# Turning a routed tile by blocks: 32 by 32 loads and a VectorE transpose in place of a TensorE transpose and a copy

## Chip, core and metric

The kernel runs on one core of a Trainium2 chip. All times are device microseconds of that core. The profile is one execution of the program with the hardware profiler on; the time before is the median of three further runs, 540.95 us (540.62 to 541.41).

## The reference

A block with two gated parts, over 8 batches of 256 tokens with 256 features, all in fp32:

```python
x = x + tanh(g_xattn) * xattn(layernorm(x), ctx)      # 16 heads of 64, 120 context rows
x = x + tanh(g_ffn) * ffn(layernorm(x))               # 8 experts, the best 2 of each token

# ffn
probs = softmax(x @ Wr.T)                    # (B, T, 8)
topk_vals, topk_idx = top_k(probs, 2)
gate = one_hot(topk_idx) weighted by topk_vals / topk_vals.sum()
h = silu(einsum('btd,efd->btef', x, W1))     # 256 -> 1024 for every expert
y = einsum('btef,edf->bted', h, W2)          # 1024 -> 256
out = einsum('bte,bted->btd', gate, y)
```

The change concerns only the way in which the expert part gets its rows.

## The kernel before

The attention part comes first: 32 units of half the heads by half a batch. Beside it the tokens of finished batches are routed. `router` finds the two best experts of each token, `places` gives each (token, expert) pair a row in a table in device memory, `routed`, which has one region of 2048 rows for each expert, and GpSimd sends the normalized token to both of its rows. A row has 265 floats: 256 features, 8 gates and the token's number, 1060 bytes.

The expert part works through `order`: eight "first" tiles, the first 128 rows of each expert's region (experts 0, 1, 2, 6, 3, 4, 5, 7 in this order), and then 23 "full" tiles, j = 8 to 30, whose expert and first row are read at run time from a small table that VectorE computes. For each tile, `load` brings 128 rows into a slot `xt` of 128 partitions by 265, one row to a partition. There are six such slots, and loads run four tiles ahead (`AHEAD`). Three other things can follow only on the slot: `turn`, the tile's gate, and the token numbers that the final addition needs.

`turn` makes the features lie on the partitions, which the first product needs: TensorE transposes each half of the tile into PSUM (two instructions, line 865) and VectorE copies both halves to `xT` in SBUF (line 867). `up` multiplies with the expert's first weights (line 874, 32 instructions of one tile) and ScalarE applies silu; `down` multiplies with the second weights (line 890, 16 instructions); VectorE scales by the gate (line 898); GpSimd adds the result to `out` through a list of row numbers (line 915). Each such addition waits for the one before it. For a full tile VectorE also copies the expert's two slabs of weights from the resident `w_sb` (lines 845 and 854) and one gate (line 850).

Small remainders of an expert's rows are worked in "quads", four lots of 32 rows to a tile; two of them run between the full tiles 16 to 23, and they keep their own load (GpSimd's gather, line 821).

The order on TensorE, VectorE, ScalarE and SyncE is the order of the program text (`manual_schedule`), so each of these engines takes its instructions strictly in turn. In the steady state an iteration i of the main loop issues, on TensorE, `up` of tile i, the turn of tile i+1, and `down` of tile i-1. On VectorE it issues the slab copy, gate copy and turn of tile i+1, then the second slab of tile i and the scaling of tile i-1.

SyncE (SP) is the queue of all tile loads of the first and full kind, and also of the stores of `x` and of the experts' weights: `load_expert(e)` sends two transfers of 1 MB (lines 407 and 410). The weights of experts 6, 5, 4, 3 and 7 can only be loaded when the attention part has left their room in `w_sb`, so they come at the change from one part to the other. In the last batch's four steps k = 0 to 3 the kernel loads the first four tiles, all at k = 0:

```python
if n == B and k == 0:
    for i in range(AHEAD):
        xts[i] = load(order[i])
```

The order on SP from there is: loads of tiles 0, 1, 2, 6; store of x of batch 6; weights of experts 6, 5, 4; load of tile 3; store of x of batch 7; load of tile 4; weights of 3 and 7; loads of tiles 5 and 7; then the full tiles. A transfer on SP carries one of eight completion semaphores in rotation, and it is issued only when the transfer eight places before it, which had the same semaphore, has landed.

Of the kernel before, what the change touches and what calls it, by code (L numbers as in the profile page):

```python
# [15 lines left out]
P = 128  # L16
B, N, D = 8, 256, 256
# [4 lines left out]
T = B * N  # L22
# [4 lines left out]
DC = D // P  # L27
# [8 lines left out]

EARLY = 2
QUARTER = 32
FULLS = 31
SPARE = 8  # L40
QUADS = 6
# [7 lines left out]
def tile_gated_xattn_moe(  # L49
# [15 lines left out]
    nc = tc.nc  # L65
# [6 lines left out]
    fp = ctx.enter_context(tc.tile_pool(name="ffn", bufs=2))  # L72
# [15 lines left out]
    routed = tc.dram_tile([E * T + P, XW], F32, name="routed")  # L88
# [35 lines left out]
    for e in range(E):  # L124
# [4 lines left out]

    places_w = const.tile([P, FULLS], F32, name="places_w")  # L130
    nc.gpsimd.iota(
        places_w, [[1, FULLS]], base=-FULLS, channel_multiplier=0,
        allow_small_or_imprecise_dtypes=True,
# [23 lines left out]
    def quarters_places():  # L157
# [4 lines left out]
        nc.vector.scalar_tensor_tensor(  # L162
            lane, quarter_i, float(-QUARTER), number[:, 0:1], ALU.mult, ALU.add
        )
# [45 lines left out]
    behind = []  # L210
    firsts = []
# [440 lines left out]
    def row(tag, n, dtype=F32):  # L652

        if tag in ("expert_i", "full_row", "quad_row", "own", "experts_i", "more_i"):
            return fw[3].tile([P, n], dtype, tag=tag, name=tag, bufs=1)
        if not scratch:
            scratch.append(fw[0].tile([P, FC * D], F32, tag="w2", name="scratch"))
            scratch.append(0)
        a, scratch[1] = scratch[1], scratch[1] + n
        r = scratch[0][:, a : a + n]  # L660
        return r if dtype == F32 else r.bitcast(dtype)
# [47 lines left out]
    def table():  # L709
# [15 lines left out]
        )  # L725
        nc.vector.tensor_scalar(tails, left, float(P - QUARTER), None, ALU.is_gt)
        nc.vector.tensor_scalar(begin[:, E:], first_row, float(P), None, ALU.add)
# [4 lines left out]

        at = row("at", FULLS)
        nc.vector.tensor_scalar(at, places_w, upto[:, 2 * E - 1 :], None, ALU.add)
        used = row("used_w", FULLS)
        nc.vector.tensor_scalar(used, at, 0.0, None, ALU.is_ge)
        yield
        which, first = sought("w", at, upto, counts, begin, P)
        full_row = row("full_row", FULLS, I32)
        where(first, used, full_row)  # L740
        expert_i = row("expert_i", FULLS, I32)
        nc.vector.tensor_scalar(used, which, float(E), float(-E), ALU.is_ge, ALU.mult)
# [5 lines left out]
        for k in range(1, 3):  # L748
            nc.vector.scalar_tensor_tensor(
                quarters, left, float(k * QUARTER), quarters, ALU.is_gt, ALU.add  # L750
            )
# [5 lines left out]
        nc.vector.tensor_scalar(used, places_q, upto_q[:, E - 1 :], None, ALU.is_lt)  # L757
        which, first = sought("q", places_q, upto_q, quarters, begin[:, :E], QUARTER)
        where(first, used, first)
# [40 lines left out]
    def take(pool, shape, tag, name, dtype=F32, **kw):  # L800
        if spare is None:
            return pool.tile(shape, dtype, tag=tag, name=name, **kw)
        key = tag, *shape
        if key not in spare:
            spare[key] = pool.tile(shape, dtype, tag=tag, name=name, **kw)
        return spare[key]


    def load(t):
        kind, i = t  # L810
        xt = take(fp, [P, XW], "xt", f"xt_{kind}{i}", bufs=6)
        if kind == "first":
            first = nc.sync.dma_start(xt, routed[ds(i * T, P), :])
            for send in behind:
                tc.declare_no_dep(
                    first.ins, send.ins, reason="rows behind those of the first tiles"
                )
            firsts.append(first)
            return xt
        if kind == "quad":  # L820
            nc.gpsimd.indirect_dma_start(
                out=xt,
                out_offset=None,
                in_=routed[:, :],
                in_offset=bass.IndirectOffsetOnAxis(
                    ap=tables[1][0][:, i : i + 1], axis=0
                ),
            )
            return xt
        start = nc.sync.value_load(  # L830
            tables[0][1][0:1, i : i + 1], min_val=0, max_val=NOWHERE
        )
        nc.sync.dma_start(xt, routed[ds(start, P), :])
        return xt

    def weights(t, xt):

# [22 lines left out]
        return w1, gate, copy_w2  # L860

    def turn(t, xt):
        tr = take(ps_tr, [P, DC, P], "tr", f"xtT_{t[0]}{t[1]}")
        for c in range(DC):
            nc.tensor.transpose(tr[:, c, :], xt[:, ts(c, P)], ident)
        xT = take(fp, [P, DC, P], "xT", f"xT_{t[0]}{t[1]}")
        nc.vector.tensor_copy(xT, tr)
        return xT
# [73 lines left out]
    def quad(j, xt):  # L942
# [30 lines left out]
        for h in range(2):  # L973
# [4 lines left out]
            for c in range(DC):  # L978
                for q in range(4):
                    nc.tensor.matmul(  # L980
                        pu[ts(q, QUARTER), :],
                        lhsT=xT[:, c, ts(q, QUARTER)],
                        rhs=w[:, q, ts(c, 512)],
# [41 lines left out]
    def open_tile(t, xt):  # L1025
        state["ready"] = t, xt, weights(t, xt), turn(t, xt)
# [11 lines left out]
    order = [("first", e) for e in (0, 1, 2, 6, 3, 4, 5, 7)]  # L1038
    order += [("full", j) for j in range(SPARE, FULLS)]
    mix = 16  # L1040
    AHEAD = 4
    xts = {}
# [35 lines left out]
    for s, (b, o, nb) in enumerate(units):  # L1078
        k = 2 * o + nb
        n = b + 1  # L1080
        g = b // 2 - 1
        routing = b > 1 and b % 2 == 1
        if s + 1 < len(units):
            prs[s + 1] = scores(units[s + 1])

        if s == 0 or k == 2 and b + 2 < B:
            norms_x.finish()
        if k == 0 and b > 1:
            norms_y.finish()
        if k == 1 and b + 2 < B:  # L1090
            if b > 1:
                xs[b + 2] = load_x(b + 2)
            norm_x(b + 2)
        if k > 1 and b > 0:
            norm_y(b - 1, k - 2)


        copies, sums = [], []
        if k == 0 and b > 0:
            weigh(b - 1, 1, ps_mm)  # L1100
        if k == 1 and routing:
            lg = logits(g, groups[g][1], bank_mm)
            next(lg)
        if k == 2:
            weigh(b, 0, ps_mm)
            if b > 0:
                sums.append(wide_out(b - 1, 1, ps_mm))
        if k == 0:
            project_q(b, xnTs[b], 3)
            if n < B:  # L1110
                project_v(b, int(b == 0))
        elif n < B:
            project_q(n, xnTs[n], k - 1)
        if k == 1:
            copies += next_k(b, 0)
            if routing and n < B:
                lg = next(lg)
            if b > 0:
                sums.append(wide_out(b - 1, 0, ps_mm))
            if routing and n == B:  # L1120
                lg = next(lg)
        if k == 3:
            copies += next_k(b, 1)
            if b > 0:
                project_v(b, 1)
            if n == B - 1:
                project_v(n, 0)
        if b == 1 and k % 2 == 0:
            copies.append(project_kk(2, k))
        for copy in copies:  # L1130
            copy()
        if s + 1 < len(units):
            divide(*prs[s + 1])
        if k == 0 and b > 1:
            turn_y(b - 2, bank_mm)


        if routing and n < B and k == 1:
            picked[g] = router(g, lg)
        for add in sums:  # L1140
            add()
        if routing and n < B and k == 2:
            sending[g] = places(g, groups[g][0], picked[g], bank_mm)
            if g == EARLY - 1:
                fill_firsts()
        if n < B:
            for step, each in list(sending.items()):
                if s < 8 * step + 18:
                    next(each)
        if s == 7:  # L1150
            quarters_places()
        if b == 0 and k == 2:
            nc.vector.tensor_scalar(bias_sb, bias_sb, tg[:, 0:1], None, ALU.mult)
        if s in (3, 4):
            bias_x(s - 3)
        if k == 1 and 0 < b < B - 1:
            bias_x(n)
        if n == B and k == 0:
            for i in range(AHEAD):
                xts[i] = load(order[i])  # L1160
        if n == B and k == 3:
            open_tile(order[0], xts[0])
            picked[g] = router(g, lg)
        turn_pr((b, o, nb), *prs.pop(s))
        if k == 3 and b + 2 < B:
            turn_x(b + 2)
        if s == 0:
            turn_x(1)
        if k == 3 and b in (2, 3, 4):
            load_expert(b - 2)  # L1170
        if k == 3 and n == B:
            load_expert(6)
# [18 lines left out]
    for i, t in enumerate(order):  # L1191
        if i == 12:

            with tc.If(more > 0):  # L1194
                spare = {}
                for j in range(SPARE):
                    tj = ("full", j)
                    xt = load(tj)
# [126 lines left out]
```

## Time and profile before

| | before |
|---|---|
| median of 3 runs | 540.95 us |
| profiled execution | 540.71 us |
| its span | 538.9 us (1.8 us lie around it) |
| TensorE busy | 525.8 us, 98% |
| VectorE busy | 285.1 us, 53% |
| ScalarE busy | 219.8 us, 41% |
| GpSimd busy | 128.7 us, 24% |
| DMA, mean share of the 16 engines, 270 to 310 us | 0.95 |
| the same, 335 to 405 us | 0.24 |

In the profile's rows, "out<-in" names the tiles written and read, "xN" counts instructions, and the number after the bar is the busy time with the mean duration of one. Durations of consecutive TensorE instructions overlap, so 46 instructions with a mean of 273 ns can be busy for 8.8 us. "Idle before" is the time that the engine stood still ahead of a group, and the name behind the arrow is what ended it. SPq is SyncE's queue; its rows show how long an issue took, and "to landing" counts from the issue to the completion.

### The profile page before, as it was taken

What the parts mean: (1) busy time and instruction counts of PE and PEld (TensorE: products, weight loads), DVE (VectorE), ACT (ScalarE), POOL (GpSimd) and SP (SyncE); (2) the same over time, 40 slices, a digit from 0 to 9 for tenths busy, and PEclk for the clock granted to TensorE, in tenths of its full rate; (3) what the DMA queues carried; (4) which work ended last, traced back from release to release, by engine and by line L of the source; (5) the groups of instructions that cost most, each with busy time, mean ns of one, the idle gap of its engine ahead of it and who ended that gap; (6) DMA issues with size and microseconds to landing.
All of it is one profiled execution on the core that took longest, in us unless ns stands there. A gap on an engine that the chain in (4) does not pass through costs nothing. (4 is left out here: it accounts for less than half of the span.)

```text
span 538.9 us, 9932 instructions
## 1 busy us (share of the span) xinstructions
PE 525.8 (98%) x3698; PEld 444.8 (83%) x3698; DVE 285.1 (53%) x683; ACT 219.8 (41%) x700; POOL 128.7 (24%) x135
## 2 busy tenths in 40 slices
PE   8999999999999999999999999999999999999992
PEld 7788887878878788787889999998997878889991
DVE  3675656567765677645663447444453453543530
ACT  1666546464664645557530311011144635501110
POOL 2011100000332003310014473222322124343422
PEclk9999999999999999999999999999999999999997
DMA  8999980140521401111099932312221210321311
GB/s 299 337 309 298 309 246 21 51 144 2 177 79 47 171 1 40 42 52 31 1 316 328 308 90 63 50 30 44 38 43 21 41 34 7 51 46 12 50 22 19
DMA packets 46439, 57.53 MB, mean 107 GB/s; under 512 B 3184, under 2 KB 41456, under 8 KB 46384
## 3 DMA queue, kind: packets, MB, share of 16 engines
q1 hardware_dynamic: 39488, 47.35, 28.6%
q0 software_dynamic: 6480, 8.81, 9.2%
q8 instruction: 32, 0.52, 0.4%
q10 hardware_dynamic: 416, 0.66, 0.4%
q14 instruction: 23, 0.19, 0.1%
HBM read 28.67 MB, written 28.27 MB: 106 GB/s over the span
## 5 line engine op out<-in xcount | busy, mean ns | idle before, releaser
L574 ACT ACTIVATE pr<-psc,mx 128x120 f32<-128x120 f32 x256 | 88.4, 372 | 64.5 <-DVE mx L568 64.5
L874 PEld LDWEIGHTS ph_full<-xT_full,w 128*128 128x128 f32 x736 | 85.0, 192 | 6.5 <-issue 5.7
L874 PE MATMUL ph_full<-xT_full,w 128*128 128x128 f32 x736 | 86.8, 276 | 0.3 <-PEq L1194 0.3
L890 PE MATMUL py_full<-w,hT_full 128*128 128x256 f32 x368 | 83.1, 379 | 0.0
L890 PEld LDWEIGHTS py_full<-w,hT_full 128*128 128x128 f32 x368 | 68.2, 190 | 8.4
L882 ACT ACTIVATE hT_full<-ph_full 128x1024 f32<-128x1024 f32 x23 | 23.5, 1023 | 97.7 <-PE ph_full L874 97.7
L524 PE MATMUL pq<-xnT,w_sb 128*128 128x256 f32 x256 | 62.7, 388 | 0.4 <-DVE xnT L207 0.4
L915 POOL DMA_INDIRECT out_dram<-y_full,xt_full x23 | 39.0, 1697 | 99.8 <-DVE y_full L898 70.4
L618 PE MATMUL pw<-w_sb 128*128 128x256 f32 x256 | 58.5, 382 | 0.0
L574 ACT ACTIVATION_READ_ACCUMULATOR pr<-psc,mx 128x1 f32 x256 | 55.7, 218 | 0.0
L524 PEld LDWEIGHTS pq<-xnT,w_sb 128*128 128x128 f32 x256 | 46.6, 190 | 10.8 <-issue 3.1
L618 PEld LDWEIGHTS pw<-w_sb 128*128 128x128 f32 x256 | 47.7, 190 | 9.0 <-issue 2.5
L562 DVE TENSOR_REDUCE mx<-psc 128x8 f32<-128x960 f32 x32 | 37.0, 1156 | 31.1 <-PE psc L554 31.1
L365 POOL DMA_INDIRECT routed<-rows,slot x32 | 32.1, 1002 | 54.4 <-DVE slot L361 47.4
L594 ACT COPY w_sb<-tr 120x512 f32<-120x512 f32 x64 | 34.6, 597 | 20.1 <-PE tr L593 20.1
L583 DVE TENSOR_TENSOR pr<-pr,sm 128x960 f32<-128x960 f32 x32 | 37.1, 1158 | 1.1
L554 PE MATMUL psc<-kT,w_sb 64*128 64x120 f32 x512 | 37.2, 284 | 0.0
L898 DVE TENSOR_SCALAR y_full<-py_full,gate 128x256 f32<-128x256 f32 x23 | 11.1, 484 | 48.5 <-PE py_full L890 44.8
L962 ACT COPY part<-w_sb 128x1024 f32 x32 | 31.1, 1043 | 14.1 <-PE py_q L1001 13.5
L554 PEld LDWEIGHTS psc<-kT,w_sb 64*128 64x128 f32 x512 | 31.1, 187 | 6.4 <-issue 3.6
L593 PEld LDWEIGHTS tr<-ident,pr 128*120 128x120 f32 x256 | 29.5, 138 | 5.5 <-issue 2.5
L845 DVE COPY w<-w_sb 128x2048 f32 x23 | 28.8, 1251 | 9.5 <-issue 4.3
(177 smaller groups left out, 670.6 us busy)
## 6 DMA issues: line engine op xcount, KB each, us to landing
routed<-w_sb SPq DMA_DIRECT2D x8, 2120.0 KB, 21.4
w_sb<-in_w1T_dram SPq DMA_DIRECT2D x8, 1024.0 KB, 5.7
w_sb<-in_w2T_dram SPq DMA_DIRECT2D x8, 1024.0 KB, 9.9
xt_full<-routed SPq DMA_DIRECT2D x23, 132.5 KB, 2.1
out_dram<-x SPq DMA_DIRECT2D x8, 256.0 KB, 2.4
x<-in_x_dram SPq DMA_DIRECT2D x7, 256.0 KB, 2.8
w_sb<-in_w_kv_dram SPq DMA_DIRECT2D x3, 512.0 KB, 8.0
xt_first<-routed SPq DMA_DIRECT2D x8, 132.5 KB, 2.5
```

The costliest lines, as they stand in the source:

```text
L365: send = nc.gpsimd.indirect_dma_start(out=routed[:, :], out_offset=bass.IndirectOffsetOnAxis(ap=slot[:, i : i + 1], axis=0), in_=rows[h][: ...
L524: nc.tensor.matmul(pq[:, i, :], lhsT=wq_sb[:, c, ts(2 * h + i, P)], rhs=xnT[:, c, :], start=(c == 0), stop=(c == DC - 1),)
L554: nc.tensor.matmul(psc[:, j, ts(i, M)], lhsT=qT[ts(j, DH), 4 * o + i, ts(nb, P)], rhs=kT[ts(j, DH), 4 * o + i, :], start=True, stop=True,)
L562: nc.vector.tensor_reduce(mx.rearrange("p (j i) -> p j i", i=4), psc[:, :, : 4 * M].rearrange("p j (i m) -> p j i m", m=M), AX.X, ALU.max,)
L574: nc.scalar.activation(pr[:, h, :], psc[:, j, ts(i, M)], AF.Exp, bias=mx[:, h : h + 1], scale=QK_SCALE, accum_out=sm[:, h : h + 1],)
L583: nc.vector.tensor_tensor(pr, pr, sm.unsqueeze(2).to_broadcast([P, 8, M]), ALU.mult)
L594: nc.scalar.copy(pT_sb[:, ts(j, 4), ts(nb, P)], tr[:M, :, :])
L618: nc.tensor.matmul(pw[:, :D], lhsT=oT_sb[b % 2][:, ci, ts(k, P)], rhs=wo_sb[:, ci, :], start=(ci == 0), stop=(ci == IC - 1),)
L874: nc.tensor.matmul(ph[:, f, :], lhsT=w1[:, c, ts(f, P)], rhs=xT[:, c, :], start=(c == 0), stop=(c == DC - 1),)
L890: nc.tensor.matmul(py[:, :D], lhsT=hT[:, f, :], rhs=w2[:, f, :], start=(f == 0), stop=(f == FC - 1),)
L915: add = nc.gpsimd.indirect_dma_start(out=out[:, :], out_offset=bass.IndirectOffsetOnAxis(ap=slots[:, k : k + 1], axis=0), in_=y[own, :], i ...
L962: nc.scalar.copy(w[:, q, :].rearrange("p (a b) -> p a b", b=D if down else DFF // 2), slab[:, ts(h, FC // 2), :] if down else slab[:, :, t ...
```

## The change

The features of a first or full tile are no longer loaded with one transfer of 128 rows. `load_blocks` issues eight transfers: for each 32 features out of each half, the 128 rows' 32 floats go to the 32 partitions on which those features will lie after the turn, as four blocks of 32 rows by 32 floats side by side. A ninth transfer brings the gates and the token numbers (9 floats) of each row. VectorE's transpose, which turns each 32 by 32 block in its place, then makes `xT` out of the slot with one instruction, SBUF to SBUF. TensorE's two transposes, the PSUM bank and the PSUM copy are gone for these tiles; quads keep them. The four loads of the last batch's k = 0 are spread: one tile's at each k.

```diff
@@ load(t)
         if kind == "first":
-            first = nc.sync.dma_start(xt, routed[ds(i * T, P), :])
-            for send in behind:
-                tc.declare_no_dep(...)
-            firsts.append(first)
+            for first in load_blocks(xt, i * T):
+                for send in behind:
+                    tc.declare_no_dep(...)
+                firsts.append(first)
             return xt
...
-        nc.sync.dma_start(xt, routed[ds(start, P), :])
+        load_blocks(xt, start)
         return xt
+
+    def load_blocks(xt, start):
+        loads = []
+        for k in range(P // BLK):
+            for c in range(DC):
+                loads.append(
+                    nc.sync.dma_start(
+                        xt[ts(k, BLK), ts(c, P)].rearrange("s (b r) -> s b r", r=BLK),
+                        routed[ds(start, P), ds(c * P + k * BLK, BLK)].rearrange(
+                            "(b s) r -> s b r", s=BLK
+                        ),
+                    )
+                )
+        loads.append(nc.sync.dma_start(xt[:, D:], routed[ds(start, P), D:]))
+        return loads
...
     def turn(t, xt):
+        if t[0] != "quad":
+            xT = take(fp, [P, DC, P], "xT", f"xT_{t[0]}{t[1]}")
+            nc.vector.transpose(xT.rearrange("p c n -> p (c n)"), xt[:, :D])
+            return xT
         tr = take(ps_tr, [P, DC, P], "tr", f"xtT_{t[0]}{t[1]}")
...
-        if n == B and k == 0:
-            for i in range(AHEAD):
-                xts[i] = load(order[i])
+        if n == B:
+            xts[k] = load(order[k])
```

`BLK` is 32. The order of VectorE's and TensorE's instructions is otherwise the same.

More of the change, by code (lines that the diff above doesn't have):

```diff
@@ L38 @@
 QUARTER = 32
+BLK = 32
 FULLS = 31
@@ L812, in load @@
         if kind == "first":
-            first = nc.sync.dma_start(xt, routed[ds(i * T, P), :])
-            for send in behind:
-                tc.declare_no_dep(
-                    first.ins, send.ins, reason="rows behind those of the first tiles"
-                )
-            firsts.append(first)
+            for first in load_blocks(xt, i * T):
+                for send in behind:
+                    tc.declare_no_dep(
+                        first.ins, send.ins, reason="rows behind those of the first tiles"
+                    )
+                firsts.append(first)
             return xt
@@ L832, in load @@
         )
-        nc.sync.dma_start(xt, routed[ds(start, P), :])
+        load_blocks(xt, start)
         return xt
+    def load_blocks(xt, start):
[9 more added lines that the diff above has]
+                    )
+                )
+        loads.append(nc.sync.dma_start(xt[:, D:], routed[ds(start, P), D:]))
+        return loads
     def weights(t, xt):
```

## The prediction

> **What bounds the kernel now.** I read the page's first part, then TensorE by stretches, then its order in one tile. TensorE is busy for 98% of the span, and by stretches it has no holes where the tiles run:
>
> ```profile
> core 0: us, PE busy (x) PEld busy (x) DVE busy (x) ACT busy (x) POOL busy (x), PEclk, DMA share, GB/s
> 270.00:310.00 40.00, 39.92 (x282) 35.38 (x281) 18.44 (x76) 10.38 (x13) 13.10 (x15) 1.00 0.95 321
> 335.00:405.00 70.00, 69.65 (x474) 64.94 (x472) 33.33 (x60) 14.13 (x14) 18.60 (x12) 1.00 0.24 40
> ```
>
> So what TensorE no longer issues shortens the kernel, as long as nothing else arrives late. The second thing to see is the DMA share: 0.95 from 270 to 310 us, where five experts' weights come in, and 0.24 in the full tiles. The change takes work from TensorE and gives it to DMA and SP. TensorE's timeline around one turn:
>
> ```profile
> 331.67 3.73 PE L874 MATMUL ph_first<-xT_first,w_sb 128*128 128x128 f32 x32
> 335.24 0.38 PE L865 MATMUL xtT_full<-ident,xt_full 128*128 128x128 f32 x2
> 335.46 3.62 PE L890 MATMUL py_first<-w_sb,hT_first 128*128 128x256 f32 x16
> ```
>
> The columns are start and duration. The next product starts 0.22 us after the two transposes did (335.24 to 335.46), although each is drawn longer: 0.22 us is what they take from the path. A plain tile lasts 7.24 us (start of `up` to start of `up`).
>
> **TensorE.** 8 first and 23 full tiles are turned, 31 x 0.22 = 6.8 us removed. Nothing on TensorE replaces it, and `up` waits for the same `xT`.
>
> **VectorE.** Out goes one PSUM copy of 128x256 (423 ns, line 867), in comes one block transpose of the same size, which the trace does not show. Bounds: 367 ns, the SBUF normalization of line 196 (0.73 us for two), and 846 ns, if it takes two passes of the 423. I take 440, nearest the copy. [...] By any of these the sum gets 0: VectorE spends some 3.5 of 7.2 us on a tile, and stood 1.7 us before each such copy, waiting for TensorE:
>
> ```profile
> L867 DVE COPY xT_full<-xtT_full 128x256 f32<-128x256 f32 x23 | 9.7, 423 | 39.6 <-PE xtT_full L865 39.5
> ```
>
> That wait (39.5 us over 23) goes; what VectorE now waits for instead is the slot's landing, with line 854's slab, the scaling of line 898 and so the addition queued behind it.
>
> **SP.** One issue of a tile becomes nine. The trace has the 128x265 load at 333 ns, a store in three dimensions (line 641) at 383 ns. For a block I take 0.38, and with the address work that each full load shows (42 + 29 + 28 ns) 0.48: 9 x 0.48 = 4.3 us, and 0.9 us for reading the row number (325.9 to 326.8): 5.2 us of SP for a full tile, 3.8 for a first tile. Less than 7.0, and SP has little else to do there; it mostly waits for slots to come free:
>
> ```profile
> SPq L833 <- DMA out_dram<-y_full,xt_full: 113.0, 14, 20.5
> ```
>
> A slot was loaded 12.5 us or more before its tile's `up` from the twelfth tile on (the tightest: 498.20 to 510.72); a load of 4.3 + 2.1 us of landing still fits.
>
> **The load on the DMA engines.** 128 packets of 1060 bytes become 1024 of 128 bytes and 128 of 36, and each transfer adds 16 small ones: 1296 in all. No row has 128 bytes. From above: the plain loads at 327 to 331 us.
>
> ```profile
> q0 software_dynamic: 145, 0.13, 24.7%
> q1 hardware_dynamic: 272, 0.26, 23.5%
> ```
>
> q1 is two tile loads: 23.5% of 16 engines x 4 us = 15.0 us for 272 packets, 55 ns each. From below: 14.0 to 15.0 us into the run, where the router's weights come in rows of 32 bytes, in two halves:
>
> ```profile
> DMA packets 287, 0.16 MB, mean 323 GB/s; under 512 B 145, under 2 KB 272, under 8 KB 287
> q1 hardware_dynamic: 287, 0.16, 110.8%
> ...
> DMA packets 205, 0.14 MB, mean 287 GB/s; under 512 B 89, under 2 KB 190, under 8 KB 205
> q1 hardware_dynamic: 205, 0.14, 121.4%
> ```
>
> They are busy for (1.108 + 1.214) x 8 = 18.6 us. Half a microsecond of large packets just before (13.0 to 13.5) took 8.4 us for 0.19 MB, 44 us a MB; 0.30 MB at that price is 13.3, and 5.3 us over 234 small packets is 23 ns. On the line from 23 ns (32 bytes) to 55 (1060) 128 bytes cost 26. So a tile takes 1296 x 26 / 16 = about 2.1 us of all engines, at most 1296 x 55 / 16 = 4.5; before it was 0.5. At 2.1 SP's issue is the slower of the two.
>
> [...]
>
> **The crowded stretch.** SP's order around the weights (start, time of issue):
>
> ```profile
> 269.57 0.39 SPq L641 DMA_DIRECT2D out_dram<-x  x1
> 270.59 0.38 SPq L407 DMA_DIRECT2D w_sb<-in_w1T_dram  x1
> ...
> 279.27 0.72 SPq L410 DMA_DIRECT2D w_sb<-in_w2T_dram  x1
> 280.03 5.13 SPq L813 DMA_DIRECT2D xt_first<-routed  x1
> 290.59 0.38 SPq L641 DMA_DIRECT2D out_dram<-x  x1
> 291.40 0.34 SPq L813 DMA_DIRECT2D xt_first<-routed  x1
> 291.80 0.44 SPq L407 DMA_DIRECT2D w_sb<-in_w1T_dram  x1
> ```
>
> Spreading the first four loads puts tile 6's nine issues behind the store at 269.57: the weights start at 273.9 instead of 270.59. Expert 4's last slab (279.27, 13.0 us to landing) then lands at 295.6 instead of 292.3. Tile 3's blocks are each eight places behind a weight transfer, the eighth behind this slab; so the store of x waits until about 296.5, tile 4's nine follow, and expert 3's first slab is issued at about 301.3 instead of 291.80. Landing like expert 6's (5.0 us), it is there at 306.3. Its product stood at 309.63 and is now due 5 x 0.22 earlier, 308.5: 2.2 us of room, no stall. Further down, the late store delays the first additions and through them GpSimd's sends, the last of which the first full load waits for (327.76 before). I estimate 1.5 us later; with 4.3 us of issues and 2.2 to landing it is there at 335.8, VectorE's turn ends at 336.4, and `up` is due at 337.1. Nearly nothing is left, so I charge 0.5 us for stalls in this stretch (0 to 3).
>
> **The end.** The additions each wait for the one before (issue 1.55, then 2.98 us idle, some 4.5). Behind the second quad they form a chain that has caught up with TensorE only at 518.92. Blocks beside them may cost 1 us; the chain has 1.77 us of room at its last link but one. Charged 0.
>
> **The sum.** 540.7 (profiled) - 6.8 + 0.5 = 534.4; the median of the runs stands 0.2 above the profiled time: 534.6.
>
> **Rivals.** (1) *Late weights.* If a tile's load takes more than about 4.5 us, that is above 55 ns a packet, the 2.2 us of room is used up three times over (tiles 6, 3 and 4 lie ahead of expert 3's slab), and the first full tiles come late too. At 5.8 us: 3 x 1.3 = 4 us more, 538.5. For it: the share of 0.95; against: 23 ns for small packets. (2) *The loads become the bound, slower than before.* The place is the full tiles: a load of L us and the additions' share (16.4% of the engines from 360 to 400 us, 1.15 us a tile) must fit in 7.0 us. Otherwise the last of 23 loads lands at 327.8 + 3 (L - 4.5) + 23 (L + 1.15), and 18 us of last products and addition follow. [...] Against: both rows above. (3) *Nothing gained.* The 6.8 us are eaten by small stalls, or the chain of additions does not move with TensorE: 541. Against: TensorE sets the last four additions' time.
>
> **How the numbers follow.** As computed 0.56 (533.2 to 536.2 its own range), rival 1 0.15 (536 to 540), rival 3 0.06, rival 2 0.23 (542 to 575). A measurement tells 0.2%, 1.1 us, from no change. Faster: 0.56 + 0.15 less 0.01 at its end, 0.70; same 0.07; slower 0.23. The range begins at 533.0 (all 6.8 us, no stall, and 1 us of spread) and reaches into rival 2 until some 0.17 is left above: 550.
>
> **What would show it.** Right: no line 865 for first and full tiles, `up` to `up` in 7.02 us, a transpose under 0.65 us, nine issues in under 5 us, a tile's packets under 30 ns. Wrong: TensorE idle before `up` of tile 3 or of full tile 8 (VectorE waiting for a load), SP's issues longer than 0.7 us each, a DMA share near 1 in the full tiles.

## The result and the profile after

The changed kernel takes 538.01 us (median; single times from 536.65 to 540.82), the kernel before 540.9 us beside it. The ratio is 0.995, with a 95% interval of 0.993 to 0.997: a gain of 2.9 us, where 6.3 were forecast. The profiled execution took 538.01 us, its span is 536.3 us.

Most of the forecast's mechanics are in the trace. TensorE by stretches, in the profile after (columns as before: busy time and instructions of each engine, granted clock, DMA share, GB/s):

```profile
270.00:310.00 40.00, 40.00 (x285) 35.84 (x284) 19.82 (x85) 10.10 (x13) 13.13 (x15) 1.00 0.85 275
335.00:405.00 70.00, 69.70 (x476) 65.21 (x474) 32.59 (x60) 14.15 (x14) 18.57 (x12) 1.00 0.33 43
```

TensorE still has no holes in these two stretches, and the loads in blocks raise the DMA share in the full tiles from 0.24 to 0.33 only. TensorE's timeline around two full tiles of the kernel after:

```profile
480.22 3.73 PE L897 MATMUL ph_full<-xT_full,w 128*128 128x128 f32 x32
483.79 3.62 PE L913 MATMUL py_full<-w,hT_full 128*128 128x256 f32 x16
487.25 3.73 PE L897 MATMUL ph_full<-xT_full,w 128*128 128x128 f32 x32
```

`up` to `up` is 487.25 - 480.22 = 7.03 us, where it was 7.24. The turn is gone from TensorE. What VectorE does in its place, from the groups of the kernel after (busy time and mean ns, then the idle time before it with its releasers), with the scaling, line 898 before and 921 after:

```profile
L884 DVE STREAM_TRANSPOSE xT_full<-xt_full 128x256 f32<-128x256 f32 x23 | 10.0, 435 | 1.1 <-DMA xt_full<-routed 0.6 <-DVE gate L869 0.3 <-issue 0.2
L898 DVE TENSOR_SCALAR y_full<-py_full,gate 128x256 f32<-128x256 f32 x23 | 11.1, 484 | 48.5 <-PE py_full L890 44.8
L921 DVE TENSOR_SCALAR y_full<-py_full,gate 128x256 f32<-128x256 f32 x23 | 11.1, 483 | 61.6 <-PE py_full L913 55.7
```

The transpose takes 435 ns. The 39.6 us that VectorE stood ahead of the copy have shrunk to 1.1 ahead of the transpose; part of that idle time now lies ahead of the scaling, which waits for `down` (61.6 us, 48.5 before). On the pages of the kernel before and of the kernel after, the queue of the loads:

```profile
q1 hardware_dynamic: 39488, 47.35, 28.6%
q1 hardware_dynamic: 75200, 47.36, 31.9%
```

The difference is 0.319 x 16 x 536.3 - 0.286 x 16 x 538.9 = 271 us of engine time for 35712 packets more: some 8 ns for each packet that came on top. That is not what one packet costs, since the large ones are gone. The durations in the trace of the kernel after give that: a packet of 128 bytes takes 14.5 ns in the mean, one of 36 bytes 10.4, one of 4 bytes (16 to a transfer) 9.1. A tile's 1024, 128 and 144 of them make 17.5 us of engine time, 13.5 ns a packet, or 1.1 us of all 16 engines.

SP's order around the weights, from its timeline in the kernel after:

```profile
274.42 0.43 SPq L852 DMA_DIRECT2D xt_first<-routed  x1
274.95 0.39 SPq L408 DMA_DIRECT2D w_sb<-in_w1T_dram  x1
...
296.81 0.40 SPq L642 DMA_DIRECT2D out_dram<-x  x1
297.25 3.86 SPq L845 DMA_DIRECT2D xt_first<-routed  x8
301.16 0.43 SPq L852 DMA_DIRECT2D xt_first<-routed  x1
301.63 0.43 SPq L408 DMA_DIRECT2D w_sb<-in_w1T_dram  x1
```

The weights start at 274.95 (forecast 273.9), the store of x at 296.81 (296.5), expert 3's first slab at 301.63 (301.3). So the gain was there. It was lost again in one place. At 322.45 TensorE was 1.97 us ahead of the kernel before (the same `up` had begun at 324.42). The timeline of the kernel before, one line, and then that of the kernel after:

```profile
324.42 3.73 PE L874 MATMUL ph_first<-xT_first,w_sb 128*128 128x128 f32 x32
...
322.45 3.73 PE L897 MATMUL ph_first<-xT_first,w_sb 128*128 128x128 f32 x32
326.07 0.59 PE L913 MATMUL py_first<-w_sb,hT_first 128*128 128x256 f32 x2
326.86 0.46 PE L913 MATMUL py_first<-w_sb,hT_first 128*128 128x256 f32 x1 [0.20 <-issue]
328.27 0.59 PE L913 MATMUL py_first<-w_sb,hT_first 128*128 128x256 f32 x2 [0.95 <-issue]
329.69 1.20 PE L913 MATMUL py_first<-w_sb,hT_first 128*128 128x256 f32 x2 [0.83 <-issue]
331.10 3.19 PE L913 MATMUL py_first<-w_sb,hT_first 128*128 128x256 f32 x9 [0.21 <-issue]
334.13 3.73 PE L897 MATMUL ph_first<-xT_first,w_sb 128*128 128x128 f32 x32
```

One `down` (16 instructions) takes 334.13 - 326.07 = 8.06 us, where it takes 3.45. That is 4.6 us lost, in the middle of a product: its operands were there, and "issue" says that TensorE waited for nothing that the profile shows. Two things go with it. ScalarE's timeline in the same place ("remote" is a releaser that the profile could not name):

```profile
331.42 1.02 ACT L905 ACTIVATE hT_first<-ph_first 128x1024 f32<-128x1024 f32 x1 [10.03 <-remote]
```

The `up` that this silu waits for ended at about 326.1; the increment of TensorE's semaphore that announces it is recorded at 331.34, 5.2 us later. VectorE runs on meanwhile without a pause, until 330.7. And the granted clock (last column but two), by windows of 2 us:

```profile
328.00:330.00 2.00, 0.91 (x3) 0.51 (x3) 1.83 (x6) 0.00 (x0) 1.70 (x2) 0.93 0.36 119
330.00:332.00 2.00, 1.79 (x4) 0.99 (x4) 0.60 (x4) 0.58 (x1) 0.57 (x1) 0.50 0.49 52
332.00:334.00 2.00, 2.00 (x8) 1.63 (x8) 0.00 (x0) 0.45 (x1) 0.00 (x0) 0.71 0.40 53
```

The trace's clock record is 0.5 from 329.735 for 3.413 us. It begins after the first pauses, and the profiles of e9, e10 and e18 below, whose stops are over 4 us, have such a window inside theirs, while no other profile has one between 300 and 345 us. So I take it for a consequence of the pauses. Inside it the products start 0.43 us apart (332.09, 332.52, 332.94), behind it 0.22 (333.26, 333.48, 333.70), so by my estimate it costs half of 3.4, about 1.7 of the 4.6 us. DMA is at less than half of its time in these windows (0.36, 0.49 and 0.40), so the engines of the transfers are not what is full.

The experiments had to find out why TensorE stops there. In what follows this is "the stop".

### The profile page after: what moved, and what is told of

It reads as the page before. It is cut to its first block, busy times and chain, and to the rows that moved or that the text cites. A ratio compares the mean times of both kernels' runs of the same rounds, so it can differ in the third digit from the quotient of the medians.

```text
span 536.3 us, 10503 instructions
## 1 busy us (share of the span) xinstructions
PE 520.9 (97%) x3636; PEld 438.5 (82%) x3636; DVE 283.9 (53%) x683; ACT 220.1 (41%) x700; POOL 127.8 (24%) x135
## 5 line engine op out<-in xcount | busy, mean ns | idle before, releaser
L921 DVE TENSOR_SCALAR y_full<-py_full,gate 128x256 f32<-128x256 f32 x23 | 11.1, 483 | 61.6 <-PE py_full L913 55.7
L985 ACT COPY part<-w_sb 128x1024 f32 x32 | 31.1, 1045 | 13.5 <-PE py_q L1024 13.0
```

What stands on the lines that cost most here:

```text
L985: nc.scalar.copy(w[:, q, :].rearrange("p (a b) -> p a b", b=D if down else DFF // 2), slab[:, ts(h, FC // 2), :] if down else slab[:, :, t ...
```

## The experiments

They were measured in five sessions: e1 to e4, e5 to e8, e9 to e12, e13 to e16, e17 and e18; the kernels of a session ran one after another on one chip, with the kernel before beside them. The theory was at first that the many small transfers cause the stop; the rival, that TensorE's shifted stream of instructions does. "None" in the table means no pause of this kind; waits for data, up to 1.65 us (e5, at the first full tile), are not counted.

| | what | us (median) | ratio to before, 95% | stop in its profile |
|---|---|---|---|---|
| e1 | plain loads, VectorE's transpose | 533.71 | 0.9848 to 0.9881 | none |
| e2 | block loads, TensorE's turn | 542.66 | 1.0025 to 1.0049 | 1.6 us |
| e3 | blocks for full tiles only | 536.02 | 0.9895 to 0.9923 | none |
| e4 | blocks for first tiles only | 544.21 | 1.0050 to 1.0076 | 1.1 us in a run of 541.02 |
| e5 | nine transfers of whole rows | 535.18 | 0.9842 to 0.9913 | none |
| e6 | tiles 5 and 7 as before | 535.14 | 0.9851 to 0.9911 | none |
| e7 | blocks for 0, 1, 2, 6 and full | 534.93 | 0.9841 to 0.9913 | none |
| e8 | first four loads at once | 534.38 | 0.9825 to 0.9898 | none |
| e9 | the changed kernel | 538.03 | 0.9935 to 0.9960 | 4.6 us |
| e10 | e4, first four at once | 544.82 | 1.0047 to 1.0076 | 5.3 us |
| e11 | e2, first four at once | 542.85 | 1.0026 to 1.0052 | 1.7 us |
| e12 | the spread alone | 540.79 | 0.9994 to 1.0012 | none |
| e13 | the changed kernel | 534.89 | 0.9880 to 0.9909 | none |
| e14 | as e8 | 534.24 | 0.9865 to 0.9894 | none |
| e15 | as e6 | 535.50 | 0.9887 to 0.9919 | none |
| e16 | as e7 | 534.59 | 0.9871 to 0.9899 | none |
| e17 | as e7 | 535.51 | 0.9885 to 0.9916 | none |
| e18 | as e8 | 536.34 | 0.9888 to 0.9920 | 4.7 us in a run of 539.89 |

The size of a stop is read from the starts of the same products on TensorE against those of the kernel before, between 320 and 341 us; it is good to some 0.2 us, since in some kernels a removed turn lies in between.

### e1: the gain without the block loads

```diff
     def load_blocks(xt, start):
+        return [nc.sync.dma_start(xt, routed[ds(start, P), :])]
```

> The changed kernel, but a first or full tile comes with one plain transfer of 128 rows as before; VectorE's transpose of the slot stays. It leaves out the placing of the features on their columns' partitions, so xT is turned only within its 32 by 32 blocks and the products are of other values; the instructions of TensorE, VectorE and ScalarE are those of the changed kernel. Theory 1 (the many small transfers of the crowded stretch hold up TensorE at 326 to 334 us): that stop is gone, 540.9 - 31 x 0.22 = about 534.1 us. Theory 2 (TensorE stops because its own instruction stream is shifted and reaches a fetch at a bad moment): the stop stays, 538 to 539 us.

Measured: 533.71 us, no stop. TensorE's, VectorE's and ScalarE's instructions are those of the changed kernel, so it is not their order that makes the stop; the rival falls. Nor is it a load of instructions that comes late: the traces have one on queue q8 near this place in every kernel, of 1.0 us at 325.99 in the result's profile, of 1.1 us at 326.44 in e13 and of 1.5 us at 327.07 in e17, and these two have no stop. And 540.8 - 533.7 = 7.1 us is what the turn's removal is worth with nothing against it (forecast 6.8).

### e2: the loads without the gain

```diff
     def turn(t, xt):
-        if t[0] != "quad":
+        if False:
```

> The changed kernel with the block loads, but TensorE's two transposes and VectorE's copy out of PSUM in place of VectorE's transpose: the cost of the loads alone. It turns blocks that are already placed, so xT holds the features in another order and the products are of other values. Theory 1 (small transfers): the stop of some 4.6 us is there, 540.9 + 4 = about 545 us. Theory 2 (TensorE's shifted stream): TensorE's stream is that of the kernel before, no stop, 541 to 541.5 us.

Measured: 542.66 us. The loads alone cost 1.9 us, less than the 4 expected. In its profile TensorE loses 1.6 us between 324 and 336 us, in small pieces.

### e3 and e4: which tiles

```diff
# e3
-        if t[0] != "quad":
+        if t[0] == "full":
...
-            for first in load_blocks(xt, i * T):
+            for first in [nc.sync.dma_start(xt, routed[ds(i * T, P), :])]:
# e4
-        if t[0] != "quad":
+        if t[0] == "first":
...
-        load_blocks(xt, start)
+        nc.sync.dma_start(xt, routed[ds(start, P), :])
```

> Block loads and VectorE's transpose for the 23 full tiles only; the eight first tiles are loaded and turned as before (one at each k, as in the changed kernel). Theory 1, by the transfers of the first tiles 5 and 7 just ahead of the stop: no stop, 540.9 - 23 x 0.22 = about 535.8 us. Theory 1, if any block load near 326 to 334 us will do (full tile 8's stand at 330): a smaller stop, 537 to 538. Theory 2: not told by it, since the stream is shifted by less.

> Block loads and VectorE's transpose for the eight first tiles only, the full tiles as before. Theory 1: TensorE gains 8 x 0.22 = 1.8 us and loses 4.6 at the stop, 543.7 us, slower than before. Theory 2: the shift is that of the changed kernel up to the stop, so the stop is there as well, 543.7. If the stop belongs to neither, 539.1 us.

Measured: 536.02 and 544.21 us. The full tiles' blocks give what was forecast for them (4.8 us for 23 x 0.22 = 5.1). The first tiles' blocks cost 3.4 us net where their turns save 1.8. The profiled execution of e4 was its shortest (541.02 us) and has a stop of 1.1 us; the other five lie between 543.1 and 544.8, so the stop varies from run to run.

### e5 to e8: what of the first tiles' loads

```diff
# e5
-        for k in range(P // BLK):
-            for c in range(DC):
-                ...
+        for k in range(8):
+            loads.append(
+                nc.sync.dma_start(xt[ts(k, 16), :D], routed[ds(start + k * 16, 16), :D])
+            )
# e6 (e7 the same with "i in (0, 1, 2, 6)")
-            for first in load_blocks(xt, i * T):
+            for first in (
+                load_blocks(xt, i * T)
+                if i not in (5, 7)
+                else [nc.sync.dma_start(xt, routed[ds(i * T, P), :])]
+            ):
# e8
-        if n == B:
-            xts[k] = load(order[k])
+        if n == B and k == 0:
+            for i in range(AHEAD):
+                xts[i] = load(order[i])
```

> The changed kernel with as many transfers and issues as before it was known that they matter: a first or full tile comes with eight transfers of 16 whole rows (1024 bytes each) and the ninth of 36 bytes; VectorE's transpose stays. It leaves out the placing of the features on their columns' partitions, so the products are of other values. Nine issues and nine completions a tile as in the changed kernel, but 128 packets of 1024 bytes in place of 1024 of 128. Theory A (the number of small packets stops TensorE): no stop, about 534 us. Theory B (the number of transfers, with SP's late order and the completions): the stop stays, 537 to 539 us.

> The changed kernel, but tiles 5 and 7, the last two first tiles, are loaded and turned as before; their loads are what SP issues just ahead of the stop. If their loads make it: no stop, 540.8 - 29 x 0.22 = about 534.4 us. If the lateness of the whole stretch makes it (tiles 6, 3 and 4 ahead of the weights): the stop stays, 537 to 539 us.

> Block loads for the first four tiles (0, 1, 2, 6, whose loads SP issues before the weights) and the full tiles; tiles 3, 4, 5 and 7 as before. If the tiles between and behind the weights make the stop: none, 540.8 - 27 x 0.22 = about 534.9 us. If the delay of the weights behind tile 6's nine issues makes it: the stop stays, 537 to 539 us.

> The changed kernel with the first four tiles' loads all at k = 0 as in the kernel before, so that SP sends the weights as early as before. If the delay of the weights and of the store of x makes the stop: most of it goes, about 534.5 us. If the blocks of tiles 3, 4, 5 and 7 make it: it stays, 537 to 539 us.

Measured: 535.18, 535.14, 534.93 and 534.38 us, and no stop in any of the four profiles. (The profiled execution of e5, 538.81 us, was 2.8 us late already at 262 us, where the change has not begun.) Taken alone this reads as three causes at once: fewer packets, no blocks for tiles 5 and 7, and an early order would each be enough. The next runs do not bear that out.

### e9 to e12: the order, and the changed kernel again

e10 and e11 put e8's edit on e4 and on e2; e12 is the kernel before with only the loads spread:

```diff
# e12
-        if n == B and k == 0:
-            for i in range(AHEAD):
-                xts[i] = load(order[i])
+        if n == B:
+            xts[k] = load(order[k])
```

> The changed kernel itself, beside e10 to e12 on one chip, because its eight single times range from 536.7 to 540.8 us and e1 to e8 were measured at other moments. If its stop belongs to the kernel: again 538 us, with a stop of 2 to 5 us in TensorE at 320 to 335 us. If the stop belonged to the moment at which it was measured: 534.5 us, as e8.

> e4 (block loads for the first tiles only), with the first four loads all at k = 0 as in the kernel before. If the spread of the first four loads makes the stop: it is gone, 540.9 - 8 x 0.22 = 539.1 us. If the blocks of the first tiles do it in any order: 543 to 544 us, as e4.

> e2 (block loads, TensorE's turn and the copy kept; products of other values), with the first four loads all at k = 0. If the spread makes e2's loss of 1.9 us: 540.9 to 541.3 us. If the loads themselves do: 542.7 us, as e2.

> The kernel before, with only the spread of the first four loads (one tile's at each k), without blocks. It puts one issue of 0.4 us more behind the store of x, so by itself nothing: 540.9 us. If the order that the spread makes is bad without blocks too: 542 us or more.

Measured: 538.03, 544.82, 542.85 and 540.79 us. The changed kernel repeats its time, and its stop too, pause by pause (a gap of 1.02 us ahead of 328.32, of 0.84 ahead of 329.76). Loading four at once gains nothing for e4 and e2, so there it is no cure, and the spread alone costs nothing. But then why did e8 have no stop?

Counting in the traces gave the hint. A transfer leaves 16 landing records (2542 for 159 transfers in the profile of the kernel before). In the profile of the changed kernel and in those of e1 to e4 and e9 to e12, 79 to 88% of them are there, also in kernels whose loads are plain (e1 88%, e12 88%). Of the changed kernel's missing ones about half lie between 284 and 332 us (586 of 1212, counted against e13's profile). In e5 to e8 and in the profile of the kernel before, over 99% are there. So these four profiles without the stop all came from a session that lost next to no records.

### e13 to e18: the kernel or the session

> The changed kernel beside the kernels of e8, e6 and e7 on one chip. If the stop belongs to the kernel: 538 us. If to the moment: as the other three, whatever that is.

> The kernel of e8 (all blocks, the first four loads at k = 0) beside the changed kernel. If the order at the loads decides: 534.4 us while the changed kernel is at 538. If the moment does: the same as the changed kernel, within 1 us.

> The kernel of e6 (tiles 5 and 7 as before) beside the changed kernel. If the blocks of tiles 5 and 7 make the stop: 535 us while the changed kernel is at 538. If the moment does: the same as the changed kernel but for 0.4 us.

> The kernel of e7 (blocks for tiles 0, 1, 2, 6 and the full tiles) beside the changed kernel. If the blocks between and behind the weights make the stop: 535 us while the changed kernel is at 538. If the moment does: the same as the changed kernel but for 0.9 us.

Measured: 534.89, 534.24, 535.50 and 534.59 us, with 99% of the records in all four. The changed kernel, not a character of it altered, is 3.1 us faster than in the result and in e9, at the same times of the kernel before (540.79 against 540.9 and 540.85). Its TensorE, where the stop was:

```profile
323.64 3.73 PE L897 MATMUL ph_first<-xT_first,w_sb 128*128 128x128 f32 x32
327.21 3.62 PE L913 MATMUL py_first<-w_sb,hT_first 128*128 128x256 f32 x16
330.67 3.73 PE L897 MATMUL ph_first<-xT_first,w_sb 128*128 128x128 f32 x32
334.24 3.62 PE L913 MATMUL py_first<-w_sb,hT_first 128*128 128x256 f32 x16
```

327.21 to 330.67 is 3.46 us for the `down` that took 8.06. What is left of losses in this profile is a wait of the kind that the prediction looked for, at the start of expert 3's tile:

```profile
309.29 3.81 PE L897 MATMUL ph_first<-xT_first,w_sb 128*128 128x128 f32 x32 [1.04 <-DMA w_sb<-in_w1T_dram]
```

e14, which sends the weights earlier, does not have it, but has one at the first full tile instead, whose load comes after the last send:

```profile
337.26 2.92 PE L897 MATMUL ph_full<-xT_full,w 128*128 128x128 f32 x24 [0.49 <-DVE xT_full L884]
```

So the same kernel has the stop in one session and not in another. e17 and e18 asked whether any of the kernels escapes the stop by itself:

> The kernel of e7 (blocks for tiles 0, 1, 2, 6 and the full tiles). In a session that loses records: about 535 us if only the blocks of tiles 3, 4, 5 and 7 bring the stop, 537 to 539 us if any block loads of first tiles do. In a session that loses none: 534.7 us.

> The kernel of e8 (all blocks, the first four loads at k = 0). In a session that loses records: 537 to 539 us, the stop of the changed kernel, if the session decides; 534.4 us if the order at the loads does. In a session that loses none: 534.3 us.

The chip lost records again here (e17 has 86%, e18 82%). e17 took 535.51 us, its four times 0.8 us apart, and TensorE is without a gap from 325 to 335 us, as the windows of e17 show:

```profile
325.00:330.00 5.00, 5.00 (x37) 4.74 (x36) 4.52 (x22) 1.02 (x1) 2.77 (x3) 1.00 0.18 58
330.00:335.00 5.00, 5.00 (x40) 4.82 (x39) 3.56 (x11) 0.07 (x1) 1.61 (x1) 1.00 0.48 54
```

e18 took 536.34 us, from 535.06 to 539.89, and the profiled execution, its slowest, has the stop. From its timeline of TensorE:

```profile
328.84 0.38 PE L913 MATMUL py_first<-w_sb,hT_first 128*128 128x256 f32 x1 [0.62 <-issue]
329.57 0.38 PE L913 MATMUL py_first<-w_sb,hT_first 128*128 128x256 f32 x1 [0.35 <-issue]
330.27 0.48 PE L913 MATMUL py_first<-w_sb,hT_first 128*128 128x256 f32 x1 [0.33 <-issue]
330.98 0.38 PE L913 MATMUL py_first<-w_sb,hT_first 128*128 128x256 f32 x1 [0.23 <-issue]
```

One product every 0.7 us, which is the step of the pauses in the changed kernel too (326.86 to 328.27 and to 329.69: twice 0.7 us each). Its other five runs lie at 535.06 to 536.99 us, all below e9's lowest (537.73), so a stop of this size is not in each of them. Whether the early order of e18 makes the stop rarer is open, as no session that loses records has both kernels.

What is shown: in the profiles, the stop is there only where two things meet. One is in the kernel, block loads for the first tiles that are loaded between and behind the weights (3, 4, 5, 7): in the sessions that lose records, e9, e10, e11, e18, e2 and e4 have them and the stop, e1, e3, e12 and e17 do not have them and have no stop. The other is the session: with over 99% of the records kept, e5, e8, e13 and e14 have nine transfers for each of these tiles and no stop. One chip was host to a session of each kind (e1 to e4 and e5 to e8), so it is not the chip alone.

What is not shown: the link between the two. The small packets and the stop do not fall together: in the result's profile the last 128-byte packet ahead of the stop starts at 323.36 us and the next at 331.68, so the queue of the loads is empty while TensorE stands, and e9 and e18 have such a gap too. The loss of records covers the place: between 317 and 331 us the result's profile has 58 landing records and e13's 392, from 332 to 336 us, when TensorE runs on again, 130 and 122. That TensorE steps at 0.7 us with its signals 5.2 us late, just where records are missing, is all that the traces have of such a link. Whether the recording has a part in the stop no run here shows: each timed run has its span and clock on record, so none tells what a run without any recording would do, and whether the stop is then there at all. Whether it is the packets or the transfers is open as well: e5, the run for that, fell into a session without the stop.

## Why the prediction was wrong

The forecast was 534.6 us; 538.0 was measured with it, and 534.9 in the session of e13. Its own steps:

- *TensorE, 6.8 us removed*: right. `up` to `up` went from 7.24 to 7.03 us (7.02 forecast), and e1, which has this step alone, gains 7.1.
- *VectorE, 440 ns, costs nothing*: right, 435 ns.
- *SP, nine issues of 0.48 us*: right in the main. A first tile's took 3.86 + 0.43 = 4.3 us against 3.8, and the work around the weights stands within 1.1 us of the forecast times. SP's idle time for free slots fell:

```profile
SPq L845 <- DMA out_dram<-y_full,xt_full: 40.2, 7, 10.3
```

- *The load on the DMA engines, 26 ns a packet*: about twice too high: 13.5 ns. The 23 ns for rows of 32 bytes, from which it came, were a remainder, after a price per MB for the large packets beside them; in the trace of the kernel before those rows take 9.0 ns each. A tile's load took 1.1 us of all engines, not 2.1. Short rows did move fewer bytes in a given time (128 in 14.5 ns, against 1024 in 48.8), but a tile has room for that. Rival 2, "the loads become the bound", fell with it; the share of 0.33 in the full tiles leaves them idle for two thirds of the time. No run shows the slow loads behind its 0.23 and its 542 to 575 us.
- *The crowded stretch, "so I charge 0.5 us for stalls in this stretch (0 to 3)"*: **this step failed.** It looked for data that come late, and there it was off by half a microsecond: 1.0 us in e13, since expert 3's first slab, issued at 301.82, took 7.5 us to land and not 5.0. What it had no term for is an engine that stops with its operands in place. That measured 4.6 us in the profile of the result (some 1.7 of them by the halved clock, as estimated above), and 0 in e13. Why TensorE stops stays open.
- *The end, charged 0*: right, the last additions follow TensorE.

With the stop, the sum is 540.7 - 6.8 + 4.6 = 538.5, against 538.0 measured; without it, with e13's wait, 540.7 - 6.8 + 1.0 = 534.9, which is what e13 measured. The range from 533.0 to 550 held the time; the likeliest case's own range (to 536.2) did not. The range held by its width, which was there for rival 2. Rival 1 named the right stretch and 538.5 us, but its cause, late weights, is worth 1 us in e13 and nothing in the result's profile; that its number comes so near is chance. What the prediction named as its refutation, TensorE idle before `up` of tile 3 or of the first full tile, did not occur in the result's profile; the time went where nobody looked, in the middle of a `down`.

A version with no stop in any of its three sessions, one of which loses records, is e7's, with blocks for the first four tiles and the full ones: 534.93, 534.59 and 535.51 us. Beside the changed kernel it ran only where that has no stop either (534.59 against 534.89, within the spread of the runs). It gives up 4 x 0.22 = 0.9 us of turns for having no small transfers in the crowded stretch.

## What to carry to other kernels

A sum over late data can be right to a microsecond and still miss a stop of an engine that waits for nothing in the profile (here 4.6 us): after a change that multiplies the transfers, look for gaps with "issue" in the middle of a product and for semaphore records that come late, ahead of building causes. Count whether a trace is complete before reading waits from it, and measure the kernel in question again beside any variant that seems to cure it; here four variants seemed to, and the unchanged kernel did as well. Where small transfers were cheap, in the quiet full tiles, I would take them (e3: 536.02 us, where the kernel before took 540.79); where transfers were crowded already, I would leave the plain load (e4, with blocks for the first tiles alone, took 544.21).

## What the runs showed that was not expected

- TensorE stopped in a product whose operands were there: 4.6 us in the result's profile, with its semaphore 5.2 us late and ScalarE waiting with it while VectorE ran on, and one product each 0.7 us in e18. Depending on the session the same kernel took 538.0 or 534.9 us, while the kernel before stayed within 540.8 to 541.2.
- The stop of the result's profile cost more than its pauses: the granted clock is 0.5 for 3.413 us inside it. In the 3.4 us before TensorE was busy for some 40% (57% in e10). The stops of 1.1 to 1.7 us in e2, e4 and e11 have no such window.
- A packet of 128 bytes took a DMA engine 14.5 ns in the mean and one of 32 bytes 9.0; the prediction had worked out 26 and 23.
